# Stage A's second input passed in with its axes exchanged, and normalized, combined and loaded in that layout

## The chip, the cores and the metric

The kernel runs on one core of a Trainium2 chip. The metric is the time of one execution on the device in microseconds (us), smaller is better. A core has a matrix engine (TensorE, "PE" in the profile; its weight loads are "PEld"), three engines for elementwise work (VectorE "DVE", ScalarE "ACT", GpSimd "POOL"), and SyncE ("SP"), which here issues all transfers between main memory and the core's own memory, in its program order.

## The reference

All data are float32. x has two inputs (b = 0, 1) of 1024 tokens with 1024 features. Four blocks follow one another, each added to what it read:

```python
x = x + attention_a(layernorm(x))   # 32 heads of 32, causal, rotary, and a small adapter of 10 tokens
x = x + ffn(layernorm(x))           # base matrix, a router over 8 experts, rank-16 experts
x = x + attention_b(layernorm(x))   # 8 heads of 16 over all tokens
x = x + ffn(layernorm(x))           # the same weights again
```

Only the first block is touched. Its projection is, for each input,

```python
qkv = einsum('btc,oc->bto', layernorm(x), w_attn)    # 1024 x 1024 times 1024 x 3072
```

layernorm subtracts the mean of a token's 1024 features and multiplies by one over the root of their variance plus 1e-5.

## The kernel before

**Stage A.** The attention of 2 inputs x 8 groups of four heads x 2 halves of the queries is written as rounds (`attend`): each round issues scores, exponentials, and the products with v. Between the rounds goes other TensorE work, the "filler": a list of generators (`Filler`), from which each round takes steps worth 1990 ns by its own reckoning (`FILL_A`; a full matmul counts 512 x 1.7 = 870). The filler of stage A is the projection of q, k and v: one `project(b, g)` for each input and group, and behind them the output projection of input 0. `project(b, g)` waits until the attention of three groups earlier is done. TensorE's and GpSimd's orders are the order in which the program text issues; VectorE's, ScalarE's and SP's are arranged by a scheduler when the kernel is built. `pin_add`, `pin_sub` and `pin` put a VectorE operation behind the latest minimum of the attention's scores.

**Chores.** Small work for other engines is put into a queue (`fill.chore`), from which each filler step takes one; `flush(key)` empties the queue up to the last one of a name.

**The projection.** The weights lie in blocks `wqk` and `wv`. The normalized input lies in memory with features on the partitions and tokens along the rows, in two halves of 512 tokens: `xnT[b, n]`, 2 MB each, two buffers ("h16"). From group 1 on, a projection is done with seven block products instead of eight (`seven`): products 1, 6, 2, 7, 5, 4, 3, four matmuls of 128x512 each. Products 6, 7 and 4 read combinations of the halves (`td`, made once by `combine` and kept in main memory), which `Stream` fetches tile by tile into a ring of five buffers ("tt"). Product 1 and 2 read half 0; 5 and 3 read half 1. `factors` makes sums of the weights on VectorE. v is projected for two groups at once (`begin_values`, `values`), products 1, 6, 2, 7 with the even group and 5, 4, 3 with the odd one.

**Input 1.** In the course of groups 1 to 5 of input 0 (the arithmetic in 2 to 5) its eight tiles of 128 tokens are loaded ("xa", three buffers), normalized on VectorE, two at the start of a group (`normalize_ahead`, `layernorm`), and stored (`xnd`). In group 7 and the first projection of input 1 they are loaded again ("t4k", three buffers), and `second` flips each tile on TensorE (L204, eight transposes of 128x128, four to a PSUM bank), from where ScalarE or VectorE copies it to `xnT[1, n]` (L232, L234). `turn_over` spreads these transposes over the filler. Group 0 of input 1 is projected plainly (`project_first`): 2 halves x k and q x 8 matmuls. After each half `combine(1)` makes the combinations: VectorE for two, GpSimd for the third.

A matmul goes through `mm`, either as one of 128 columns (L198) or, between two rounds, as four of 32 columns side by side (L200).

Of the kernel before, what the change touches and what calls it, by code (L numbers as in the profile page):

```python
# [20 lines left out]
P = 128  # L21
B, T, C = 2, 1024, 1024
NT = T // P
# [18 lines left out]


AHEAD = "ahead"
WAIT = "wait"
# [102 lines left out]
def tile_model(ctx: ExitStack, tc: tile.TileContext, d, out: bass.AP):  # L148
# [92 lines left out]
    def layernorm(pl, tag, x, name, behind=False, then=None):  # L241
# [16 lines left out]
        e = pl.tile([P, 1], F32, tag="e0", name=f"e_{name}", bufs=2)  # L258
        xn = pl.tile([P, C], F32, tag=tag, name=f"xn_{name}")

        def rest():
            r = dve.tensor_scalar(e, r0, r0, ve, ALU.mult, ALU.mult)
            if behind:
                pin(r)
            dve.tensor_scalar(e, e, -0.5, 1.5, ALU.mult, ALU.add)
            dve.tensor_scalar(r0, r0, e, None, ALU.mult)
            dve.tensor_scalar(xn, x, mv[:, 0:1], r0, ALU.subtract, ALU.mult)  # L267
            if then is not None:
                then()
# [316 lines left out]

    xnd = [dram.tile([P, C], F32, name=f"xnd{t}") for t in range(NT)]

    def stage_a(wk, big):
# [46 lines left out]
        class Stream:  # L636


            def __init__(self, b, order):
                self.b, self.todo, self.here = b, deque((i, c) for i in order for c in range(4)), deque()  # L640
                self.fetch()

            def fetch(self):
                while self.todo and len(self.here) < RING:
                    i, c = self.todo.popleft()
                    t = big.tile([P, HF], F32, tag="tt", name=f"tt{self.b}_{i}_{c}_{len(self.todo)}")
                    sp.dma_start(t, td[self.b, i, c])
                    self.here.append(((i, c), t))

            def get(self, i, c):  # L650
                self.fetch()
                at, t = self.here.popleft()
                assert at == (i, c)
                return t

        streams = {}

# [5 lines left out]
        def combine(b):  # L663

            ts = {}
            for c in range(4):
                b11, b12, b21, b22 = (block(b, i)[:, c, :] for i in (11, 12, 21, 22))
                fill.chore(("T", b), lambda c=c, x=b22, y=b12: made(ts, b, 3, c, pin_sub, x, y))
                fill.chore(("T", b), lambda c=c, y=b11: made(ts, b, 2, c, pin_add, ts[3, c], y))
                fill.chore(("T", b), lambda c=c, y=b21: made(ts, b, 4, c, in_pieces(pool.tensor_sub), ts[2, c], y))  # L670

            order = []
            for g in range(NG):
                order += [2, 3, 4] if g else []
                if g > 1 or b:
                    order += [4] if g % 2 else [2, 3]
            fill.chore(("T", b), lambda: streams.update({b: Stream(b, order)}))

# [13 lines left out]
        def seven(b, nm, f, mul, shape, c, first, settled):  # L692
# [3 lines left out]
            right = {1: lambda k: block(b, 11)[:, k, :], 2: lambda k: block(b, 21)[:, k, :], 3: lambda k: block(b, 22)[:, k, :],  # L696
                     4: lambda k: streams[b].get(4, k), 5: lambda k: block(b, 12)[:, k, :],
                     6: lambda k: streams[b].get(2, k), 7: lambda k: streams[b].get(3, k)}

# [58 lines left out]

        def normalize_ahead():

            xs = {t: x_load(1, t, big, "xa") for t in range(2)}
            yield ("norm", -1)
            for t in range(NT + 1):
                if t:
                    settle(f"a1_{t - 1}")
                    sp.dma_start(xnd[t - 1], xn)
                if t + 2 < NT:
                    xs[t + 2] = x_load(1, t + 2, big, "xa")
                if t < NT:
                    xn = layernorm(big, "t4k", xs.pop(t), f"a1_{t}", behind=True)  # L770
                yield ("norm", t)

        def second():


            def load(t):
                xn = big.tile([P, C], F32, tag="t4k", name=f"xn1_{t}")
                sp.dma_start(xn, xnd[t])
                return xn

            xns = {t: load(t) for t in range(2)}
            for t in range(NT):
                n, i = divmod(t, 4)
                if i == 0:
                    yield None
                    xnT[1, n] = big.tile([P, NC, HF], F32, tag="h16", name=f"xnT1_{n}")
                if t + 2 < NT:
                    xns[t + 2] = load(t + 2)
                yield from transposed(xns.pop(t), xnT[1, n][:, :, i * P : (i + 1) * P], f"a1_{t}")

        given = [False]
        owed = [0]

        def turn_over():

            owed[0] += 1
            if given[0]:
                given[0] = False
                return
            while owed[0]:  # L800
                owed[0] -= 1
                yield next(turnover)

        def adapter_scores(u):
            given[0] = True
            b, g, n = u.at
# [32 lines left out]
        def late(r, begun):  # L839
            spent = 0.0  # L840
            given[0] = False
            for u, at in begun.items():
# [51 lines left out]
        def project(b, g, between=None):  # L894
# [5 lines left out]
            for key in "kq":  # L900
                st[key, b, g] = wk.tile([P, T], F32, tag="qk", name=f"{key}T{nm}")
            if g == 0:
                yield from project_first(b, between)
            else:
                yield from project_blocks(b, g)
            del wqk_at[b, g]
            if g and ng and nb < B:
                yield from begin(nb, ng)
            if (b, g) != (0, 0) and (b, g) != (0, 1):
                yield from values(b, g)  # L910

        def project_first(b, between):
            wqk = wqk_at[b, 0]
            if b == 0:
                yield adapter_parts("k0", lambda c: wqk[:, c, 1, :], P)
            else:
                assert next(turnover) is None
                yield from begin_values(b, 0)
            for n in range(2):
                if n == 1:  # L920
                    if b == 0:
                        yield from between
                    yield from begin(b, 1)
                    combine(b)
                xh = xnT[b, n]
                for s, key in ((1, "k"), (0, "q")):
                    qp = next_bank([P, HF], f"{key}p{b}_{n}")
                    for c in range(NC):
                        mm(qp, lhsT=wqk[:, c, s, :], rhs=xh[:, c, :], start=(c == 0), stop=(c == NC - 1))
                        yield HF * COL  # L930
                        if b and n == 0 and c % 2:
                            yield from turn_over()
                    rotate(b, 0, key, n, qp)
                    if b == 0 and n == 0 and key == "k":
                        yield adapter_keys(0)
                if b and n == 0:
                    while owed[0]:
                        owed[0] -= 1
                        yield next(turnover)
                yield ("qk", b, 0, n)  # L940
                if b == 0:
                    yield from values_first(n)
            combine_first(b)

        def project_blocks(b, g):
            nm = f"{b}_{g}"
            k, q = st["k", b, g], st["q", b, g]
            if (b, g) == (0, NG - 1):
                assert next(turnover) is None
            halves = {i: (t, n) for i, t, n in ((11, k, 0), (12, k, 1), (21, q, 0), (22, q, 1))}  # L950
# [10 lines left out]
            for r in seven(b, nm, st.pop(("f", b, g)), mul, [P, HF], places, lambda x: rotate(b, g, "k", 0, x), settled):  # L961
# [5 lines left out]
                else:  # L967
                    yield r
                    i += 1
                    if i == 14 and b == 0:  # L970
                        yield adapter_keys(g)
                    if (b, g) == (0, NG - 1) and i > 12 and i % 2 == 0:
                        yield from turn_over()
            while owed[0]:
                owed[0] -= 1
                yield next(turnover)
            yield ("qk", b, g, 1)
# [97 lines left out]
        fill.add(half(0, 0, xns))  # L1075
        ahead = normalize_ahead()
        turnover = second()
        for b in range(B):
            for g in range(NG):

                old = b * NG + g - 3
                if b == 0 and g >= 1:
                    fill.add(ahead_of(ahead, 2 if g > 1 else 1))
                fill.add(project(b, g, half(0, 1, xns) if b == g == 0 else None),
# [10 lines left out]
        return wp  # L1095

    def ahead_of(gen, n):
        for _ in range(n):
            r = next(gen, None)
            if r is not None:  # L1100
                yield r

# [533 lines left out]
    with tc.manual_schedule(engines={mybir.EngineType.PE}):  # L1636
        with tc.tile_pool(name="big", bufs=2, side="left", reuse_waits="tile") as bigp:
            psa = ExitStack()
            ps = psa.enter_context(tc.tile_pool(name="psA", bufs=1, space=bass.MemoryType.PSUM, reuse_waits="tile"))
            big = PoolOf(bigp, {"h16": 2, "t4k": 3, "xa": 3, "tt": RING, "wqk": 2, "wv": 1})  # L1640
            with tc.tile_pool(name="wkA", bufs=5, side="right", reuse_waits="tile") as wk:
# [163 lines left out]
```

## Time and profile before

| | |
|---|---|
| median of three runs | 2345.24 us (2343.0 to 2349.63) |
| the profiled execution | 2345.64 us, of which the profile's span is 2343.9 |
| TensorE busy | 2287.6 us (98%) |
| VectorE, ScalarE, GpSimd busy | 1435.9, 1090.6, 600.0 us |
| mean granted TensorE clock | 0.996 |
| projection and attention of stage A | about 19 to 1295 us; the hand-over from input 0 to input 1 near 580 us |

A line of the table by stretch gives start:end, length, then for PE, PEld, DVE, ACT and POOL the busy time with the number of instructions in brackets, then the granted clock (1.00 is full speed), the busy share of the transfer engines and GB/s. A line in order of time gives start, duration, engine, line of the program, operation, what it writes and reads, shapes, the number of instructions run together, and in square brackets how long the engine stood idle before it and for whom it waited. A line of the chain of waits gives start, duration and what. Lines of "PE" have modelled ends, so costs of matmuls are taken from start to start.

### The profile page before, as it was taken

To read this page: it belongs to the slowest core of one execution; us is meant where nothing else is said; L and a number is where in the kernel's file an instruction comes from. 1 tells how busy PE (TensorE), PEld (TensorE's weight loads), DVE (VectorE), ACT (ScalarE), POOL (GpSimd) and SP (SyncE) were. 2 spreads that over 40 slices of the span, in tenths; PEclk is the share of its full clock that TensorE was granted. 3 is DMA by queue.
4 is the path that set the end of the run, shared out by engine and by line. 5 is a ranking of instruction groups with operands and counts; after the bars stand their busy time and mean duration, and the time that the engine had idled before them with its cause. 6 is when DMAs were issued, how large, how long until landed. Compare 5 with 4: busy or idle time off the path is not lost.

```text
span 2343.9 us, 61203 instructions
## 1 busy us (share of the span) xinstructions
PE 2287.6 (98%) x25221; PEld 1048.8 (45%) x25221; DVE 1435.9 (61%) x4365; ACT 1090.6 (47%) x2090; POOL 600.0 (26%) x933
## 2 busy tenths in 40 slices
PE   8999999999999999999999999999999999999999
PEld 4435443455354443445433445566433553233454
DVE  7586766666656666566661246567766765675453
ACT  3356665666565665666652000012455545665100
POOL 1432232222233232222302114302111111222322
PEclk9999999999999999999999999999999999999999
DMA  5443334333243333332322574442332302323543
GB/s 175 151 140 117 121 102 129 110 96 111 88 124 110 103 98 108 91 111 80 128 73 78 192 249 171 157 144 79 127 104 84 118 19 73 117 82 112 180 161 123
DMA packets 182968, 277.37 MB, mean 118 GB/s; under 512 B 19488, under 2 KB 85152, under 8 KB 182688
## 3 DMA queue, kind: packets, MB, share of 16 engines
q1 hardware_dynamic: 182688, 273.46, 36.1%
q8 instruction: 197, 3.23, 0.6%
q14 instruction: 83, 0.68, 0.1%
HBM read 215.19 MB, written 55.57 MB: 116 GB/s over the span
## 4 chain that ended last, share of the span: by engine, by line
PE 87%; DVE 8%; DMA 3%; ACT 1%; issue 1%; POOL 0%; SPq 0%; DVEq 0%; POOLq 0%; ACTq 0%
PE st L411 9%; PE sc L339 7%; PE y_A L433 6%; PE y L200 6%; PE y_f L198 5%; PE x L200 4%; PE z_f L198 4%; PE z L200 4%; PE st L409 3%; PE y_v L200 3%; PE x_f L198 3%; PE y_B L433 2%; PE y_f L200 2%; PE y_p L198 2%; PE x_v L200 2%; PE hp_f L198 2%
## 5 line engine op out<-in xcount | busy, mean ns | idle before, releaser
L545 ACT ACTIVATE pt<-st 128x1024 f32<-128x1024 f32 (+1 forms) x418 | 424.0, 1019 | 559.7 <-PE st L411 433.3
L360 ACT ACTIVATE pr_A<-pr_A,nmax_A 128x896 f32<-128x896 f32 (+7 forms) x512 | 390.0, 765 | 43.5 <-DVE nmax_A L352 42.7
L352 DVE CUSTOM_DVE_ANT_0 pr_A<-sc,mask 128x512 f32<-128x512 f32 (+3 forms) x512 | 250.3, 536 | 179.0 <-PE st L411 96.4
L339 PE MATMUL sc<-kT,qT 32*128 32x512 f32 (+3 forms) x1536 | 319.3, 522 | 5.6 <-POOL qT L884 2.7
L411 PE MATMUL st<-qT,kT 32*128 32x512 f32 (+3 forms) x1536 | 297.0, 487 | 0.0
L352 DVE CUSTOM_DVE_ANT_0 pr_A<-sc,mask,part_A 128x512 f32<-128x512 f32 (+1 forms) x256 | 156.3, 648 | 146.5 <-PE sc L339 94.2
L418 POOL TENSOR_SCALAR_AFFINE_SELECT pt<-pt 128x256 f32<-128x256 f32 x256 | 104.4, 425 | 452.6 <-ACT pt L545 451.8
L239 POOL TENSOR_TENSOR xf<-xf,b_base 128x256 f32<-128x256 f32 x100 | 74.8, 779 | 413.4 <-DVE xn_f L267 288.4
L360 ACT ACTIVATE pr_B<-pr_B,nmax_B 128x1024 f32<-128x1024 f32 x128 | 145.5, 1140 | 35.4 <-DVE nmax_B L352 35.4
L433 PE MATMUL y_A<-pt,v 128*32 128x512 f32 (+3 forms) x1536 | 158.5, 498 | 1.8 <-issue 1.8
L339 PE MATMUL sc<-kq,qk 32*128 32x512 f32 x512 | 134.3, 643 | 6.6 <-DVE nmax_B L352 5.2
L411 PEld LDWEIGHTS st<-qT,kT 32*128 32x128 f32 x1536 | 129.1, 185 | 15.2 <-issue 10.7
L411 PE MATMUL st<-rows_B,kq 32*128 32x512 f32 x512 | 134.0, 640 | 1.1 <-ACT pt L545 0.8
L409 PE MATMUL st<-rows_A,ones 3*128 3x512 bf16 (+3 forms) x768 | 123.3, 329 | 4.7 <-DVE nmax_A L352 2.2
L352 DVE CUSTOM_DVE_ANT_0 pr_B<-sc,zeros,part_B 128x512 f32<-128x512 f32 x128 | 91.0, 747 | 51.8 <-PE sc L339 51.6
L409 PEld LDWEIGHTS <-ones 3*128 3x128 bf16 x768 | 35.9, 91 | 186.5 <-issue 181.0
L883 POOL TENSOR_TENSOR qr<-qr,sin 128x256 f32<-128x256 f32 x64 | 62.2, 972 | 220.2 <-DVE qr L879 213.4
L339 PEld LDWEIGHTS sc<-kT,qT 32*128 32x128 f32 x1536 | 109.9, 184 | 15.6 <-POOL qT L884 4.7
L352 DVE CUSTOM_DVE_ANT_0 pr_B<-sc,zeros 128x512 f32<-128x512 f32 x128 | 83.5, 686 | 52.9 <-PE sc L339 52.7
L200 PE MATMUL x<-xnT,wqk 128*32 128x512 f32 x896 | 109.6, 602 | 0.0
L200 PE MATMUL y<-tt,wqk 128*32 128x512 f32 x864 | 104.3, 594 | 0.0
L360 ACT ACTIVATION_READ_ACCUMULATOR pr_A<-pr_A,nmax_A 128x1 f32 x512 | 97.2, 190 | 0.0
(407 smaller groups left out, 4088.9 us busy)
## 6 DMA issues: line engine op xcount, KB each, us to landing
tt<-td SPq DMA_DIRECT2D x252, 256.0 KB
qkb_f<-tf SPq DMA_DIRECT2D x96, 256.0 KB
qkb_s<-tf SPq DMA_DIRECT2D x84, 256.0 KB
wqk<-in_w_attnT SPq DMA_DIRECT2D x32, 512.0 KB
xf<-x SPq DMA_DIRECT2D x25, 512.0 KB
xa<-in_x SPq DMA_DIRECT2D x16, 512.0 KB
wv<-in_w_attnT SPq DMA_DIRECT2D x8, 1024.0 KB
yd<-ys SPq DMA_DIRECT2D x32, 256.0 KB
```

Source lines behind the costliest of these rows:

```text
L198: return pe.matmul(out, lhsT=lhsT, rhs=rhs, start=start, stop=stop, skip_group_check=True)
L200: pe.matmul(out[i : i + 32], lhsT=lhsT[:, i : i + 32], rhs=rhs, start=start, stop=stop, skip_group_check=True)
L239: pool.tensor_add(dst[:, i : i + 2 * P], a[:, i : i + 2 * P], b[:, i : i + 2 * P])
L339: yield w * COL, lambda: pe.matmul(dst[:, o : o + w], lhsT=self.qt[rows, qc : qc + P], rhs=self.kt[rows, c0 : c0 + w], start=True, stop=True)
L352: minimum[0] = dve.tensor_tensor_reduce(pr[:, c0 : c0 + w], sc[:, i, o : o + w], m, -self.scale, BIG if c0 == 0 else self.part[:, col], AL ...
L360: tc.keep_in_program_order(act.activation(pr[:, :nk], pr[:, :nk], AF.Exp, bias=self.nmax[:, col], scale=-1.0, accum_out=self.sums[:, col]))
L409: yield w * COL / 4, lambda: pe.matmul(dst[:, o : o + w], lhsT=of["ones"][three, :], rhs=self.rows[three, off : off + w], start=True, stop ...
L411: yield w * COL, lambda: pe.matmul(dst[:, o : o + w], lhsT=self.kt[rows, kb * P : (kb + 1) * P], rhs=rhs, start=self.extra, stop=True)
L418: pool.affine_select(out=dg, in_=dg, compare_op=ALU.is_ge, fill=0.0, base=0, pattern=[[0, 2], [1, P]], channel_multiplier=-1)
L433: pe.matmul(self.y[32 * h : 32 * h + 32, off : off + w], lhsT=self.value(h, kb), rhs=pt[h // 2][:, h % 2, o : o + w], start=self.opens, st ...
L545: act.activation(pt[:, :, low_:wide_], st[:, :, low_:wide_], AF.Exp, scale=ts[0][0].scale)
L883: pool.tensor_mul(qr[:, hs], qr[:, hs], sin[:, cols][:, hs])
```

## The change

Input 1 is also passed in as `x1T`, its 1024 x 1024 values with features first. The eight loads by tokens stay, for mean and variance alone: `layernorm` with no tag ends with the two columns, which go to main memory (`moments`) in stores of 128 values. When all are there, they are loaded as two rows spread over all partitions ("mo", two tiles of 128x1024). Then, in four blocks c, two tiles of 128 features (c and c + 4, 128x1024 each) are loaded from `x1T` into "t4k"; VectorE subtracts the mean, GpSimd multiplies by the factor, and the three combinations for input 1 and the difference that product 5 needs are made there, one chore at each filler step; all are stored (`td`, `xnd`). The loads of block c + 1 are issued at the end of block c. `AHEAD_AT` says how many steps of this generator go ahead of a group's projection of q and k and how many behind it.

`second(n)` only loads: half 0 of input 1 into the buffer of half 0 of input 0 when product 2 of group 7 has read it, half 1 behind the last v product of group 7. There are no transposes, no copies and no `turn_over`. Group 0 of input 1 is projected in the seven-product form, and its first v products follow it like those of other even groups. One `Stream` runs over both inputs. "xa" (three buffers of 4 KB a partition) is gone; "mo" (two of 4 KB) and "z4" (one of 2 KB) are new.

```diff
+AHEAD_AT = {g: n for g, n in enumerate(((0, 0), (2, 0), (2, 2), (2, 1), (1, 1), (1, 1), (1, 1), (0, 0)))}
...
         def rest():
...
             dve.tensor_scalar(r0, r0, e, None, ALU.mult)
+            if xn is None:
+                then(mv[:, 0:1], r0)
+                return
             dve.tensor_scalar(xn, x, mv[:, 0:1], r0, ALU.subtract, ALU.mult)
...
-        def normalize_ahead():
...
+        def moments_ahead():
+            xs = {t: x_load(1, t, big, "t4k") for t in range(2)}
             yield ("norm", -1)
+            for t in range(NT):
                 if t + 2 < NT:
+                    xs[t + 2] = x_load(1, t + 2, big, "t4k")
+                def keep(mean, r, t=t):
+                    for i, v in enumerate((mean, r)):
+                        sp.dma_start(moments[i, t * P : (t + 1) * P].rearrange("(p o) -> p o", o=1), v)
+                settle(f"a1_{t - 2}")
+                layernorm(big, None, xs.pop(t), f"a1_{t}", behind=True, then=keep)
                 yield ("norm", t)
+            settle(f"a1_{NT - 1}")
+            mean, r = (big.tile([P, T], F32, tag="mo", name=f"moments{i}") for i in range(2))
+            for i, v in enumerate((mean, r)):
+                sp.dma_start(v, moments[i].partition_broadcast(P))
+            at = []
+            def load(c):
+                for k in (c, c + 4):
+                    x = big.tile([P, T], F32, tag="t4k", name=f"xc{k}")
+                    sp.dma_start(x, d["x1T"][k * P : (k + 1) * P, :])
+                    at.append(x)
+            load(0)
+            yield ("norm", NT)
+            for c in range(4):
...
+                for x, cols in places:
+                    chore(lambda x=x, cols=cols: pin_sub(x[:, cols], x[:, cols], mean[:, cols]))
+                for x, cols in places:
+                    chore(lambda x=x, cols=cols: in_pieces(pool.tensor_mul)(x[:, cols], x[:, cols], r[:, cols]))
+                    if x is hi:
+                        n = int(cols is right_)
+                        chore(lambda n=n, cols=cols, hi=hi: sp.dma_start(xnd[n, c + 4], hi[:, cols]))
+                chore(lambda: sp.dma_start(xnd[0, c], lo[:, left]))
+                chore(lambda: pin_sub(z[:, left], hi[:, right_], lo[:, right_]))
+                chore(lambda: pin_add(z[:, right_], z[:, left], lo[:, left]))
+                chore(lambda: in_pieces(pool.tensor_sub)(z4, z[:, right_], hi[:, left]))
+                chore(lambda: pin_sub(lo[:, right_], lo[:, right_], lo[:, left]))
+                def keep(c=c, lo=lo, z=z, z4=z4):
+                    sp.dma_start(td[1, 3, c], z[:, left])
+                    sp.dma_start(td[1, 2, c], z[:, right_])
+                    sp.dma_start(td[1, 4, c], z4)
+                    sp.dma_start(xnd[1, c], lo[:, right_])
+                    if c < 3:
+                        load(c + 1)
+                chore(keep)
+                yield ("norm", NT + 1 + c)
+                fill.flush("xc")
...
+        def second(n):
+            xnT[1, n] = big.tile([P, NC, HF], F32, tag="h16", name=f"xnT1_{n}")
+            for c in range(NC):
+                sp.dma_start(xnT[1, n][:, c, :], xnd[n, c])
...
-                yield from transposed(xns.pop(t), xnT[1, n][:, :, i * P : (i + 1) * P], f"a1_{t}")
...
             for key in "kq":
                 st[key, b, g] = wk.tile([P, T], F32, tag="qk", name=f"{key}T{nm}")
-            if g == 0:
-                yield from project_first(b, between)
+            if b == 0 and g:
+                yield from ahead_of(AHEAD_AT[g][0])
+            if b == g == 0:
+                yield from project_first(between)
             else:
                 yield from project_blocks(b, g)
             del wqk_at[b, g]
-            if g and ng and nb < B:
+            if (b or g) and nb < B:
                 yield from begin(nb, ng)
+            if b == 0 and g:
+                yield from ahead_of(AHEAD_AT[g][1])
             if (b, g) != (0, 0) and (b, g) != (0, 1):
                 yield from values(b, g)
+            if (b, g) == (0, NG - 1):
+                second(1)
...
-                    if (b, g) == (0, NG - 1) and i > 12 and i % 2 == 0:
-                        yield from turn_over()
+                    if (b, g) == (0, NG - 1) and i == 13:
+                        second(0)
...
-            big = PoolOf(bigp, {"h16": 2, "t4k": 3, "xa": 3, "tt": RING, "wqk": 2, "wv": 1})
+            big = PoolOf(bigp, {"h16": 2, "t4k": 3, "mo": 2, "z4": 1, "tt": RING, "wqk": 2, "wv": 1})
...
+        "x1T": a[A + "x"][1].T,
```

## The prediction

> **What bounds the kernel now.** I read the totals first, then the table by stretch, then the instructions in order of time on TensorE and VectorE, then the chain of waits around the hand-over from input 0 to input 1. The totals:
>
> ```profile
> PE 2287.6 (98%) x25221; PEld 1048.8 (45%) x25221; DVE 1435.9 (61%) x4365; ACT 1090.6 (47%) x2090; POOL 600.0 (26%) x933
> ```
>
> TensorE is the bound, and only 56 us are not its own. So an edit pays by the TensorE work it removes and by the gaps it closes, and it costs by the gaps it opens. The table by stretch shows where stage A has gaps (columns: length, then busy time of each engine, then granted clock):
>
> ```profile
> 125.00:145.00 20.00, 16.27 (x192) 5.62 (x188) 18.65 (x67) 9.17 (x33) 9.82 (x12) 1.00 0.65 215
> 195.00:216.00 21.00, 19.18 (x316) 9.66 (x306) 17.14 (x66) 14.62 (x41) 4.18 (x8) 0.92 0.37 117
> 276.00:296.00 20.00, 18.58 (x251) 7.31 (x244) 15.79 (x57) 12.97 (x33) 3.70 (x9) 1.00 0.56 193
> 355.00:376.00 21.00, 19.19 (x258) 7.88 (x254) 14.20 (x54) 11.86 (x28) 3.58 (x8) 0.92 0.62 205
> 376.00:440.00 64.00, 64.00 (x1000) 29.08 (x996) 40.91 (x131) 39.23 (x79) 19.43 (x30) 1.00 0.35 106
> 580.00:604.00 24.00, 18.42 (x192) 8.37 (x187) 12.18 (x38) 8.54 (x18) 2.91 (x8) 0.93 0.24 78
> ```
>
> The first four are the places where two layernorms of input 1 are pushed through VectorE. Their gaps are 3.73, 1.82, 1.42 and 1.81 us, and in two of them the clock of 0.92 costs another 21 x 0.08 = 1.7 us: 12.1 us in all, 3.0 for a pair. Between them, as in 376 to 440, TensorE never stops. The last row is the hand-over: 5.58 us idle and 24 x 0.07 = 1.7 us of clock.
>
> **Removed: 64 transposes on TensorE.** They come in 16 groups of four, one in nearly every round of attention:
>
> ```profile
> 539.71 1.07 PE L433 MATMUL y_A<-pt,v 128*32 128x512 f32 x8
> 540.70 0.66 PE L204 MATMUL xt_a<-ident,xn 128*128 128x128 f32 x4
> 541.20 1.02 PE L198 MATMUL z<-xnT,s 128*128 128x512 f32 x2
> ```
>
> From start to start a group takes 0.50 us, and the work ahead of it ends 0.11 us later than where no transpose follows (0.99 against 0.88 us for the same eight matmuls at 546.96). I take 0.60; a group behind a full-width matmul (559.13 to 559.57) took 0.44. So 16 x 0.60 = 9.6 us, at least 7.0. TensorE is never waiting for someone else there, so this is on the path.
>
> **Removed: four matmuls.** Group 0 of input 1 goes from 32 full matmuls to 28 of the seven-product form. Eight such matmuls take 3.43 us, so 4 x 0.43 = 1.7 us.
>
> **Removed: the stall at the hand-over.** Today the v weights of (1, 0) are loaded at 581.4, and the sums made of them stand next in VectorE's queue:
>
> ```profile
> 581.40 5.02 DMA wv<-in_w_attnT
> ```
> ```profile
> 582.19 0.68 DVE L730 TENSOR_TENSOR v<-v,z_v 128x512 f32<-128x512 f32 x1
> 586.44 0.69 DVE L227 TENSOR_TENSOR s_v<-wv 128x512 f32<-128x512 f32 x1 [3.57 <-DMA wv<-in_w_attnT]
> ```
> ```profile
> 589.03 0.63 PE L204 MATMUL xt_a<-ident,xn 128*128 128x128 f32 x4 [2.48 <-issue]
> 590.55 1.03 PE L204 MATMUL xt_a<-ident,xn 128*128 128x128 f32 x4 [0.89 <-DVE xnT L232]
> 598.36 0.66 PE L204 MATMUL xt_a<-ident,xn 128*128 128x128 f32 x4 [2.22 <-DVE rows_A L232]
> ```
>
> VectorE stands still for 3.57 us, and everything behind it (the copies of the transposes, the minima, rows_A) is late; TensorE loses 5.58 + 1.7 = 7.3 us. After the change the sums come behind 16 filler steps and there are no copies. A round of attention takes 3.9 us (624.43 to 628.33) and is given 1990 ns of filler at 870 for a step, 2.3 steps: 1.7 us a step, 27 us for the 16. The wait is covered. If it were not, 7.3 us stay. Removed in all: 18.6 us.
>
> [...] The rows decide: after a gap of 1.81 us at 204.7 the four us from 206 to 210 ran at 0.70.
>
> **Moved: the layernorms of input 1.** The statistics stay, the 0.81 us normalization on VectorE goes. A pair then costs 5.1 instead of 6.7 us of VectorE time. With 3.0 x 5.1 / 6.7 = 2.3 for each of four pairs it is 9.2 instead of 12.1: -2.9 us (between 0, if they crowd, since all are now done before group 4, and -6.4, if each pair falls to the cheapest, 1.42).
>
> **Added: four blocks of combination work**, one chore for each filler step, from the middle of group 4 to the start of group 6. Together 28 VectorE operations of 0.69 us (19.3) and 40 GpSimd pieces of about 0.75 us (30); gone are 7 copies, 8 normalizations and 8 sums on VectorE, 7 copies net on ScalarE. VectorE's sum rises by some 8 us with the nine operations of the new seven-product group, which lie where VectorE idles for TensorE (57.8 us busy of the 96 from 604 to 700). A block is 4.8 us of VectorE time; in one heap it would cost 3.0 x 4.8 / 6.7 = 2.2, but it is strung over some 27 us. I take 1.2 (between 0 and 3.5, the dearest later pair): 4.8 us.
>
> What speaks against it is that GpSimd slows VectorE where both work:
>
> ```profile
> 124.06 0.67 DVE L726 TENSOR_TENSOR qT<-qT,y 128x512 f32<-128x512 f32 x1
> 126.72 1.22 DVE L880 TENSOR_TENSOR qT<-qT,cos 128x512 f32<-128x512 f32 x1
> ```
>
> The second ran beside a GpSimd product (1.16 instead of 0.73 us). If all 28 ran so, they would add 28 x 0.54 = 15 us to VectorE, and a block would be 8.6 us, more than a pair: then 3.5 each. I hold 1.2, as most subtracts come before the products of their block.
>
> [...]
>
> **Added: waits for the new loads.** x1T comes as two 512 KB loads for each block into t4k's three slots, which the block before still fills; so block c+1 is loaded only when block c has stored. Blocks 0 and 2 follow their loads by 28 and 12 filler steps: no wait. Block 1 starts with the very step at which its load is issued (block 0 gets 19 chores and 17 steps). On SP ahead of that load stand a tt load that waits for TensorE, six awT transfers (0.53 to 0.66 us each, 3.6 us), a td store waiting for GpSimd; then it lands in 3.37 (512 KB, first x load of the chain) to 5.02 us (1 MB, above): 8.0 to 9.6 us. VectorE gets there after a round (3.9 us) and three operations, about 6 us: it waits 2 to 3.6 us. Queued behind it are the minima of the next round, for which ScalarE's exponentials wait, and for them TensorE, which has two sc buffers. By the hand-over's row: 3.0 us idle and 1.7 of clock, 4.7 us (0 to 7.3). Block 3 has one attention round and the four tail chores between load and use: 1.5 us (0 to 7.3). Together 6.2.
>
> **Added: SP's queue.** 54 more issues (16 small stores of mean and 1/deviation, 8 x1T loads, 2 broadcasts, 16 half loads for 8 whole ones, and so on), some 0.4 us each: 22 us over 400, no bound. But a store that waits for GpSimd holds the tt loads behind it. The ring of five covers about 8 steps, 14 us. Ends: 0, and 2.65 us for each block (the longest tt wait in the chain, at 150.71). I take 1.0 in all. The half loads of xnT at the hand-over go out 27 steps (half 0) and 16 steps (half 1) before use, against 15 us for 3 MB with the v weights at the 5.02 us row's rate; the tt load behind half 0 has 14 us for about 11.5: 0.5 us (0 to 2.65).
>
> **Sum.** -18.6 - 2.9 + 4.8 + 6.2 + 1.0 + 0.5 = -9.0 us. The profiled execution took 2345.64 us (span 2343.9), 0.4 above the median of 2345.24. So 2336.6 us.
>
> **The rivals.** *All gain:* blocks and loads hide, only the first two terms stand: -21.5, 2324.1 us. For it: 376 to 580 has 0.25 us of gap in 204. Against it: block 1's load.
> *No difference:* GpSimd stretches all VectorE work, blocks at 3.5 each (14.0 instead of 4.8): +0.2, 2345.8 us. For it the 1.22 row, against it that VectorE is idle a third of that time.
> *Slower:* each of the four blocks holds VectorE for its load as the v weights did, 4 x 7.3 = 29.2 instead of 6.2: +14.0, 2359.6 us. It decides once more than three of them wait in full (load waits over 22 us). Against it: the 28 and 12 steps ahead of blocks 0 and 2.
> That the transposes are not really gone is no rival: the changed program issues none for input 1.
>
> **How the numbers follow.** Chances: forecast 0.45 (2330 to 2342), all gain 0.17, no difference 0.22, slower 0.16. Under 0.3% (7 us, about what a measurement of this kernel tells from no change) counts as same; a sixth of the forecast's case lies there. Faster 0.38 + 0.17 = 0.55, same 0.07 + 0.22 = 0.29, slower 0.16. The range, 2324 to 2352, takes in the first three cases with their ends and leaves out most of the slower one.
>
> **What would show it.** Right: no gap around the hand-over, no xt_a group behind the start; one gap of 2 to 4 us at the start of group 5 (near 360 us), where VectorE waits for xc; small ones at groups 2 and 3. Wrong: VectorE waits for xc in all blocks, TensorE waits for tt or xnT, or the 128x512 subtracts last over 1 us and gaps line the stretch from 320 to 480.

## The result, and the profile after

The changed kernel takes 2366.8 us (median of 4 runs, 2359.09 to 2368.54), the kernel before 2347.24 beside it: a ratio of 1.0079, with a 95% interval of 1.0051 to 1.0107. It is slower by 20 us. The profiled execution took 2368.54 us, its span is 2366.8, the mean granted clock 0.988 (before 0.996). The totals of the page after:

```profile
PE 2287.3 (97%) x25263; PEld 1047.7 (44%) x25263; DVE 1448.4 (61%) x4378; ACT 1088.9 (46%) x2083; POOL 617.7 (26%) x957
```

TensorE's busy time is the same to 0.3 us, although the transposes are gone; the granted clock is lower, and with it back at 0.998 the best version below has 2267.4. The idle time rose from 56.3 to 79.5 us. The table by stretch, with the stretches of the prediction and, below them, two more:

```profile
125.00:145.00 20.00, 18.03 (x205) 6.01 (x200) 18.67 (x71) 9.97 (x35) 9.20 (x12) 0.91 0.90 137
195.00:216.00 21.00, 16.01 (x343) 10.71 (x342) 8.63 (x35) 12.86 (x29) 1.59 (x4) 0.92 0.58 90
276.00:296.00 20.00, 18.48 (x433) 12.00 (x428) 14.96 (x51) 12.15 (x25) 5.82 (x8) 1.00 0.59 96
355.00:376.00 21.00, 20.76 (x454) 12.71 (x448) 17.86 (x52) 14.37 (x31) 9.50 (x14) 1.00 0.38 110
376.00:440.00 64.00, 56.55 (x772) 23.56 (x768) 40.40 (x116) 32.95 (x63) 25.99 (x40) 0.92 0.50 165
580.00:604.00 24.00, 24.00 (x226) 6.94 (x218) 13.95 (x39) 13.51 (x22) 6.82 (x9) 1.00 0.46 150
145.00:195.00 50.00, 43.95 (x611) 17.62 (x604) 35.02 (x105) 22.89 (x46) 14.32 (x19) 0.93 0.56 99
480.00:500.00 20.00, 11.41 (x80) 3.85 (x83) 12.70 (x28) 5.83 (x10) 9.04 (x14) 0.66 0.37 124
```

The stall at the hand-over (580 to 604) is gone, as forecast. The stretch from 376, gapless before, now has 7.45 us of gap, and the one from 195 has 4.99 instead of 1.82. TensorE's larger gaps, in order of time (the bracket is the idle time ahead of the line and who ended it; one of 2.04 us at 235.79, behind VectorE, is left out):

```profile
153.85 3.64 PE L201 MATMUL y<-tt,wqk 128*32 128x512 f32 x16 [4.38 <-DMA tt<-td]
200.00 3.58 PE L201 MATMUL x_v<-wv,xnT 128*32 128x128 f32 x62 [2.98 <-issue]
251.49 1.93 PE L201 MATMUL y<-tt,wqk 128*32 128x512 f32 x8 [3.92 <-DMA tt<-td]
304.26 3.21 PE L201 MATMUL z_v<-wv,xnT 128*32 128x128 f32 x54 [5.18 <-issue]
400.21 1.22 PE L343 MATMUL sc<-kT,qT 32*128 32x512 f32 x2 [7.45 <-DVE part_A L356]
486.64 0.40 PE L413 MATMUL st<-rows_A,ones 3*128 3x256 bf16 x2 [6.81 <-DVE nmax_A L356]
490.68 0.39 PE L413 MATMUL st<-rows_A,ones 3*128 3x256 bf16 x2 [1.95 <-DVE rows_A L233]
```

They are of two kinds. Up to 305 us TensorE waits for combination tiles (tt) or for nothing that the profile shows ("issue"). At 400 and 487 it waits for VectorE, and VectorE waits for the x1T loads of blocks 1 and 3:

```profile
398.08 0.69 DVE L225 TENSOR_TENSOR xc<-xc,moments 128x512 f32<-128x512 f32 x1 [7.86 <-DMA xc<-in_x1T]
481.86 0.69 DVE L225 TENSOR_TENSOR xc<-xc,moments 128x512 f32<-128x512 f32 x1 [8.16 <-DMA xc<-in_x1T]
```

SyncE's queue ahead of the first of these loads (start, duration of the issue) and the chain of waits ahead of the second (start, duration, what) say why they are late:

```profile
388.66 0.55 SPq L868 DMA_DIRECT2D awTA<-adbA  x1
...
391.79 0.66 SPq L869 DMA_DIRECT2D awTA<-adbA  x1
392.54 0.38 SPq L817 DMA_DIRECT2D td<-xz  x1
392.97 1.86 SPq L788 DMA_DIRECT2D xc<-in_x1T  x2
```
```profile
469.34 7.36 DMA wv<-in_w_attnT
476.70 0.02 issue
476.72 5.02 DMA xc<-in_x1T
```

The first kind stands where the sixteen stores of means and factors are issued (92 to 290 us). Transfers are slow there: the chain of waits has one of the adapter's weights, 16 KB or less, that took 12.54 us. It spans the gap ahead of 153.85 and lands after it, so it is a neighbour of the late tt load and not its cause:

```profile
142.87 12.54 DMA awTA<-adbA
```

From 190 to 196 us, around two of the stores, the transfer engines are busy for 74% of the time and move 37 GB/s (last two columns):

```profile
190.00:196.00 6.00, 5.28 (x100) 2.57 (x94) 1.88 (x8) 1.03 (x1) 0.00 (x0) 1.00 0.74 37
```

A fixed mark serves for what follows: the last of the 32 stores of attention results (yd), where stage A's attention ends, at 1296.3 us before (first line) and at 1323.9 after (second).

```profile
L1046 SPq DMA_DIRECT2D yd<-ys x32: 319/378/834, 120.2 to 1296.3; - x32
L1066 SPq DMA_DIRECT2D yd<-ys x32: 319/376/982, 121.0 to 1323.9; - x32
```

Stage A lost 27.6 us. What follows took 1047.6 us before and 1042.9 after, with the same instructions; in the other profiled runs below it took 1038.4 to 1052.2. So a few us of a difference between whole times need not come from stage A; where a stage A price is wanted, the mark is better. The stores are counted from 0 here. Store 8 came 56.4 us later than before (510.2 against 453.8), store 16 only 26.6 later: 29.8 us of gains are there, behind larger losses. A store in the middle is a rougher mark than the last one, as it also moves with how much filler goes ahead of it.

### The profile page after: what moved, and what is told of

It reads as the page before. It is cut to its first block, busy times and chain, and to the rows that moved or that the text cites. A ratio compares the mean times of both kernels' runs of the same rounds, so it can differ in the third digit from the quotient of the medians.

```text
span 2366.8 us, 61406 instructions
## 1 busy us (share of the span) xinstructions
PE 2287.3 (97%) x25263; PEld 1047.7 (44%) x25263; DVE 1448.4 (61%) x4378; ACT 1088.9 (46%) x2083; POOL 617.7 (26%) x957
## 4 chain that ended last, share of the span: by engine, by line
PE 85%; DVE 7%; DMA 4%; ACT 2%; issue 1%; POOL 0%; SPq 0%; DVEq 0%; POOLq 0%; ACTq 0%
PE st L415 9%; PE sc L343 7%; PE y L201 6%; PE y_A L437 6%; PE y_f L199 4%; PE z L201 4%; PE x L201 4%; PE z_f L199 4%; PE st L413 3%; PE y_v L201 3%; PE x_f L199 3%; PE y_B L437 2%; PE y_f L201 2%; PE y_p L199 2%; PE z_v L201 2%; PE x_v L201 2%
## 5 line engine op out<-in xcount | busy, mean ns | idle before, releaser
L201 PE MATMUL y<-tt,wqk 128*32 128x512 f32 x960 | 118.9, 606 | 8.3 <-DMA tt<-td 8.3
L201 PE MATMUL x<-xnT,wqk 128*32 128x512 f32 x960 | 120.5, 614 | 0.0
L343 PEld LDWEIGHTS sc<-kT,qT 32*128 32x128 f32 x1536 | 110.6, 185 | 18.6 <-DVE part_A L356 8.0
```

Of the source, the lines that this page charges most:

```text
L201: pe.matmul(out[i : i + 32], lhsT=lhsT[:, i : i + 32], rhs=rhs, start=start, stop=stop, skip_group_check=True)
L343: yield w * COL, lambda: pe.matmul(dst[:, o : o + w], lhsT=self.qt[rows, qc : qc + P], rhs=self.kt[rows, c0 : c0 + w], start=True, stop=True)
```

## The experiments

Two theories. **T1:** the sixteen stores of 128 elements of 4 bytes clog the transfers, and tt, awT and instructions come late. **T2:** blocks 1 and 3 hold VectorE for loads that are issued too late. The rivals are crowded layernorms, a longer SyncE queue, and GpSimd slowing VectorE.

**One gathered store** (gather). The columns go to one tile, TensorE flips it, one store writes 16 rows of 512 bytes:

```diff
-    sp.dma_start(moments[i, t * P : (t + 1) * P].rearrange("(p o) -> p o", o=1), v)
+    dve.tensor_copy(cols[:, i * NT + t : i * NT + t + 1], v)
...
+            ct = bank([2 * NT, P], "colsT")
+            flip(ct, cols, ident)
+            rows = wk.tile([2 * NT, P], F32, tag="colsT", name="colsT_sb", bufs=1)
+            act.copy(rows, ct)
+            sp.dma_start(moments.rearrange("i (t p) -> (i t) p", p=P), rows)
```

> The changed kernel, but the means and factors of the eight layernorms are copied into sixteen columns of one SBUF tile, flipped once by TensorE and stored once as 16 rows of 512 bytes, instead of sixteen stores of 128 elements of 4 bytes. T1 (the small stores clog the DMA queues, and the tt and awT transfers and TensorE's instructions come late): the four gaps at 153.9 (4.38 us), 200.0 (2.98), 251.5 (3.92) and 304.3 (5.18) shrink to under 1.5 us each, awT and tt transfers in 125 to 300 land in under 5 us, and about 18 us of idle time and 8 us of clock go: some 2341 us where the changed kernel takes 2367. The gaps of 7.45 and 6.81 us at 400 and 487 stay. Rival (the pairs of layernorms crowd each other in groups 1 to 3, or SP has too many issues): the gaps stay, less than 5 us goes.

Measured: 2341.88 us, ratio to before 0.9979 (0.9971 to 0.9988); the four gaps are gone, the two others stay. T1 holds, 24.9 us below the changed kernel. The rivals of crowding and of SyncE's other new issues fall: those are all still there. TensorE's gaps over 0.9 us from 135 to 480 are now these:

```profile
182.42 0.39 PE L413 MATMUL st<-rows_A,ones 3*128 3x512 bf16 x2 [1.40 <-DVE part_A L356]
205.14 0.39 PE L413 MATMUL st<-rows_A,ones 3*128 3x512 bf16 x2 [1.22 <-DVE rows_A L233]
262.32 0.39 PE L413 MATMUL st<-rows_A,ones 3*128 3x512 bf16 x2 [1.51 <-DVE nmax_A L356]
368.87 1.22 PE L343 MATMUL sc<-kT,qT 32*128 32x512 f32 x2 [7.24 <-DVE part_A L356]
455.01 0.40 PE L413 MATMUL st<-rows_A,ones 3*128 3x256 bf16 x2 [6.38 <-DVE nmax_A L356]
459.05 0.40 PE L413 MATMUL st<-rows_A,ones 3*128 3x256 bf16 x2 [1.96 <-DVE rows_A L233]
```

**Blocks further apart** (spread). Only the values in the table of steps are changed:

```diff
-((0, 0), (2, 0), (2, 2), (2, 1), (1, 1), (1, 1), (1, 1), (0, 0))
+((0, 0), (3, 0), (2, 2), (2, 1), (1, 1), (0, 1), (0, 1), (1, 0))
```

> The changed kernel with the small stores kept, but the four combination blocks start at least 16 filler steps after their loads are issued (steps of the work ahead for groups 1 to 7: (3,0) (2,2) (2,1) (1,1) (0,1) (0,1) (1,0)). T2 (blocks 1 and 3 hold VectorE because the x1T load is issued with the step that uses it): VectorE no longer waits for xc, the gaps of 7.45 at 400 and of 6.81 and 1.95 at 487 go, and with the clock about 22 us: some 2345 us. Rival (GpSimd and VectorE slow each other in the blocks, and the gaps would be there with early loads too): gaps of 4 us or more stay at two blocks, and less than 8 us goes.

Measured: 2342.45 us, 0.9977 (0.9968 to 0.9986), 24.4 below the changed kernel. From 360 to 500 us VectorE waits for no load, and TensorE has no gap over 0.9 us behind 260. T2 holds. The gaps ahead of 260 stay, as the small stores do. The rival of GpSimd slowing VectorE falls: VectorE operations stretched beside GpSimd are still there, and no gap follows. One of them, and two stretches:

```profile
387.93 1.21 DVE L225 TENSOR_TENSOR xc<-xc 128x512 f32<-128x512 f32 x1
```
```profile
380.00:400.00 20.00, 20.00 (x330) 9.36 (x324) 15.22 (x50) 13.17 (x28) 7.28 (x14) 1.00 0.64 216
420.00:480.00 60.00, 60.00 (x988) 28.80 (x984) 43.73 (x132) 37.51 (x77) 28.67 (x44) 1.00 0.49 154
```

**Both** (both).

> One gathered store and spread blocks together. If T1 and T2 are the two causes and they are independent: 27 + 22 us less than the changed kernel, some 2318 us, 29 us below the kernel before, TensorE idle about 35 us. If one of them falls, the time is that of the other alone (2341 or 2345). If my forecast's remaining terms are right (-18.6 - 2.9 + 4.8 + 0.5, load waits at 0) it is 2329.

Measured: 2324.86 us, 0.991 (0.9897 to 0.9924): 22.7 us below before. Of the 27 + 22 expected, 42 came. Part of the rest is a gap that the gathering itself makes, where TensorE's flip waits for VectorE:

```profile
259.35 0.28 PE L205 MATMUL colsT<-ident,cols 128*16 128x128 f32 x1 [3.72 <-DVE parts_k L233]
```

**The flip later** (best). The same kernel, with the flip, its store and the broadcast loads as a chore five filler steps later:

```diff
+            for run in [lambda: None] * 5 + [gather]:
+                fill.chore("cols", run)
...
+            fill.flush("cols")
```

> The kernel with the gathered store and the spread blocks, with the flip of the sixteen columns, its store and the two broadcast loads five filler steps later, so that TensorE doesn't stand for 3.72 us at 259 behind VectorE's adapter copy. T: the gap goes and with it 216:276's clock of 0.97: 4 to 5.5 us, some 2320 us. Rival (the broadcast loads come too late for block 0 and VectorE waits for them): no gain or a loss of up to 3 us.

Measured: 2313.79 us, 0.987 (0.9852 to 0.9889). The gap is gone and the stretch's clock is back at 1.00:

```profile
216.00:276.00 60.00, 59.73 (x964) 27.69 (x951) 40.08 (x125) 38.21 (x75) 18.80 (x30) 1.00 0.37 113
```

By the mark it is 7.2 us ahead of the kernel with both (1267.5 against 1274.7), 5.5 of them already at store 3; the other 3.9 of the 11.1 between the medians are not in stage A's attention, and behind it the two have the same instructions.

```profile
L1078 SPq DMA_DIRECT2D yd<-ys x32: 319/380/1410, 120.3 to 1267.5; - x32
```

Against the changed kernel the mark moved by 56.4 us. T1 alone moved it by 32.5 (1291.4), T2 alone by 23.9 (1300.0): the two add up to the 56.4, which are the 27.6 lost and 28.8 gained on the kernel before. This version is 33 us faster than the kernel before and 53 faster than the changed one.

**The small stores alone, in the kernel before** (b_small). To a place that nobody reads:

```diff
                     sp.dma_start(xnd[t - 1], xn)
+                    for i in range(2):
+                        sp.dma_start(extra[i, t - 1, 0, :].rearrange("(p o) -> p o", o=1), last[f"a1_{t - 1}"][i])
```

> The kernel before, with two stores of 128 elements of 4 bytes added after each of the eight layernorms of input 1 (sixteen in all, the mean and the factor, to a place in DRAM that nobody reads); nothing else changed. T1: the stores alone cost 15 to 27 us, 2362 to 2374 us, with gaps of 3 us and more in 100 to 560 on TensorE that wait for tt or for instructions. Rival (the stores are harmless, as my forecast has it with at most 1 us): within 3 us of the kernel before.

Measured: 2396.96 us, 1.0216 (1.0202 to 1.023): +49.4, beyond the range. That is 49.4 / 16 = 3.1 us each, where the changed kernel's cost 24.9 / 16 = 1.6. These stores are spread over 123 to 412 us and may meet more tt loads; that was not tried. The chain of waits has a tt load of 256 KB that took 18.73 us, and TensorE's longest gap is the last line:

```profile
138.17 18.73 DMA tt<-td
156.89 0.04 issue
156.94 1.93 PE y L200 x8
```
```profile
346.71 1.93 PE L200 MATMUL y<-tt,wqk 128*32 128x512 f32 x8 [12.89 <-DMA tt<-td]
```

**What about them costs?** Four kernels with other sixteen stores at the same places (only the destination and the source of each store are given; a row of `extra` has 128 elements in b_far4 and 16 in b_step64):

```diff
-  extra[i, t - 1, 0, :].rearrange("(p o) -> p o", o=1), last[...][i]    # b_small: 128 x 4 B, side by side
+  extra[i, t - 1], xn[:, i * P : (i + 1) * P]                           # b_rows: 128 x 512 B
+  extra[i, t - 1], xn[:, i * 16 : (i + 1) * 16]                         # b_near64: 128 x 64 B, side by side
+  extra[i, t - 1][:, 0:1], last[...][i]                                 # b_far4: 128 x 4 B, 512 B apart
+  extra[i, t - 1][:, 0:1], last[...][i]                                 # b_step64: 128 x 4 B, 64 B apart
```

> The kernel before with sixteen added stores at the same places as the small ones, but each of 128 rows of 512 bytes (a slice of the normalized tile, 64 KB) to a place in DRAM that nobody reads. If the element size of 4 bytes is what costs, these stores with 128 times the bytes cost far less than the 49.4 us of the small ones: under 6 us, 2347 to 2354 us. If the number of issues or of rows, or SP's waiting behind a store, is what costs, they cost about the same: 2390 us or more.

> The kernel before with the sixteen added stores of 128 elements of 4 bytes, but each element goes to a row of its own, 512 bytes from the next, where the first such kernel put the 128 elements side by side. If the neighbourhood costs (many writers of one 512-byte stretch of DRAM wait for each other): under 8 us more than the kernel before. If the small element by itself costs: about the same 49 us, 2390 us or more.

> The kernel before with sixteen added stores of 128 rows of 64 bytes (sixteen columns of the normalized tile), side by side in DRAM, 8 KB each. If anything below 512 bytes costs like the 4-byte elements: about +49 us. If the cost belongs to elements of 4 bytes side by side, or falls with the size: under 10 us.

> The kernel before with the sixteen added stores of 128 elements of 4 bytes, each element 64 bytes from the next in DRAM. If the writers that hold each other up share a stretch of 64 bytes or less, these share none: under 8 us more than the kernel before, as with 512 bytes between them. If the shared stretch is longer (512 bytes, say), eight elements still fall into one: well over 10 us more, up to the 49 of side by side.

| sixteen stores, each of 128 pieces | median, us | ratio to the kernel before, run beside each |
|---|---|---|
| 4 B, side by side | 2396.96 | 1.0216 (1.0202 to 1.023) |
| 4 B, 64 B apart | 2347.31 | 1.0005 (0.9995 to 1.0016) |
| 4 B, 512 B apart | 2345.59 | 0.9996 (0.9985 to 1.0006) |
| 64 B, side by side | 2349.19 | 1.0006 (0.9994 to 1.0018) |
| 512 B, side by side | 2346.17 | 1.0 (0.9991 to 1.0009) |

T1 as I had put it, the 4-byte element, falls in part. Number of stores, of rows, small size and SyncE's issues cost nothing that can be measured here; of the five forms only the one with several elements within 64 bytes does (side by side there are sixteen in each such stretch; spacings between 4 and 64 bytes were not tried). The stretch from 136 to 160 us, first of the 4-byte elements side by side, then of those 512 B apart: fewer bytes, twice the share of the transfer engines.

```profile
136.00:160.00 24.00, 16.86 (x180) 6.19 (x174) 14.40 (x57) 10.96 (x34) 3.73 (x6) 0.89 1.04 144
```
```profile
136.00:160.00 24.00, 23.56 (x296) 7.67 (x292) 21.64 (x76) 14.29 (x41) 4.59 (x8) 0.97 0.51 161
```

If small size were what costs, the 64 B stores (2349.19 us) and the spaced 4 B stores (2347.31 and 2345.59) would have cost too. What happens in the memory when several elements go to one such stretch, no run here shows.

**From another queue** (act_small). In the changed kernel ScalarE issues the sixteen stores (`act.dma_start` for `sp.dma_start`).

> The changed kernel with its sixteen 4-byte-element stores issued from ScalarE instead of SyncE; nothing else changed. If the stores hold up what stands behind them in SyncE's queue alone: the tt gaps of 4.38 at 154 and 3.92 at 251 shrink, and 15 to 25 us of the 25 that the gathered store won are won here too, 2342 to 2352 us. If they clog the DMA engines for every queue: within 6 us of the changed kernel's 2366.8, and instruction fetches still come late.

Measured: 2367.65 us, 1.0086 (1.0068 to 1.0104), the changed kernel's time. So SyncE's order is not what holds the tt loads up. The gap at 251 is gone, but others came: one for tt at 111 (2.70 us), and the "issue" gap near 300 grew from 5.18 to 6.05.

```profile
154.33 3.90 PE L201 MATMUL y<-tt,wqk 128*32 128x512 f32 x16 [2.63 <-issue]
298.50 3.21 PE L201 MATMUL z_v<-wv,xnT 128*32 128x128 f32 x54 [6.05 <-issue]
```

This run has the small stores in a queue of their own, and shows that they do not fill the transfer engines themselves. Queue, packets, MB and share of the 16 engines' time, first of this run (SyncE's queue, then ScalarE's with the sixteen stores), then of SyncE's queue with the gathered store:

```profile
q1 hardware_dynamic: 188160, 281.85, 39.5%
q10 hardware_dynamic: 2304, 0.01, 0.1%
```
```profile
q1 hardware_dynamic: 188192, 281.86, 37.7%
```

The small stores' packets take 0.1%, 9 ns each in the median; SyncE's other packets, of the same bytes, take 1.8% more. In the traces' records of single packets, 109 in the changed kernel, 115 in spread, 136 here and 175 in b_small lasted over 2.5 us, nearly all of them packets of other transfers; none did in the ten kernels without such stores. A packet of 2 KB takes 84 ns in the median in all of them. So single packets of other transfers last up to 8.6 us in the changed kernel while these stores are about. What they wait for is not recorded.

**The hand-over alone** (b_late_wv). In the kernel before, the sums of the v weights wait until the first half is projected:

```diff
             for n in range(2):
                 if n == 1:
+                    if b:
+                        yield from begin_values(b, 0)
```

> The kernel before, with the seven-product sums of the v weights of input 1, group 0 placed after the first half's projection instead of ahead of it, some 16 filler steps after their load; nothing else changed. My forecast's term: VectorE's 3.57 us standstill at 582 goes, and TensorE's gaps of 2.48 and 2.22 us with it and the lowered clock: -7.3 us, 2340 us. Rival (the gaps there come from the transposes' copies and the start of the new input, whatever the weights do): less than 2 us.

Measured: 2347.15 us, 1.0005 (0.9995 to 1.0014): no gain, though VectorE's wait for wv at 582 (3.57 us) is gone. Store 12 comes at 607.0 instead of 611.8, 4.8 us ahead. Of the two gaps that I ascribed to that wait, the first is gone, the second is not (first line); and by store 13 the 4.8 are given back (664.6 against 663.0), at 640 to 665, where products now meet late minima and tt loads and the clock is 0.86. By the whole time the rival of my forecast holds.

```profile
593.59 0.66 PE L204 MATMUL xt_a<-ident,xn 128*128 128x128 f32 x4 [2.21 <-DVE rows_A L232]
647.86 0.70 PE L339 MATMUL sc<-kT,qT 32*128 32x512 f32 x2 [1.93 <-DVE nmax_A L352]
652.62 1.08 PE L200 MATMUL y_v<-s_v,tt 128*32 128x128 f32 x32 [1.41 <-DMA tt<-td]
654.85 1.93 PE L200 MATMUL y_v<-s_v,tt 128*32 128x128 f32 x32 [1.15 <-DMA tt<-td]
```

**The transposes' price** (both_flips). Dummy transposes in the kernel with both:

```diff
+   if (b, g) in ((0, NG - 1), (1, 0)) and i > 12 and i % 2 == 0:
+       pt = bank([P, 4, P], f"again_{b}_{i}")
+       for j in range(4):
+           flip(pt[:, j, :], ident, ident)
+       yield 440.0
```

> The kernel with the gathered store and the spread blocks, and sixteen groups of four transposes of the identity put in where the kernel before has its own for input 1 (group 7 of input 0 and the first projection of input 1), their results read by nobody. My forecast's price is 0.60 us a group: +9.6 us (7.0 at the least), 2334.5 us. Rival (TensorE has slack between the halves of a round, and the removed transposes gave less): under +4.

Measured: 2325.68 us, 0.9914 (0.9899 to 0.9929), only 0.8 above both. By whole times my price would fall. By the marks it stands: stores 16 to 20 come 8.8 to 9.9 us later than without the flips, 0.55 to 0.62 for a group, and the last store 7.0 later, my lower end. What lies behind stage A took 1038.4 us in this profile and 1049.3 in that of both. The difference is the clock and the gaps there, as the stretch from 1900 to 2300 us shows, first of both, then of this run:

```profile
1900.00:2300.00 400.00, 387.94 (x2584) 151.57 (x2585) 222.68 (x642) 165.19 (x264) 99.08 (x136) 0.98 0.36 119
```
```profile
1900.00:2300.00 400.00, 391.06 (x2639) 153.71 (x2640) 227.38 (x656) 169.16 (x269) 103.05 (x142) 1.00 0.36 120
```

TensorE idles 12.1 us in the first and 8.9 in the second, and 400 x 0.02 = 8 us go to the clock in the first alone. What lowers the clock there in one run and not in the other is open, so the price is shown for stage A, and not as a change of the whole time.

## Why the prediction was wrong

**The step that failed first: "SP's queue", "16 small stores ... some 0.4 us each ... no bound", 1.0 us in all.** I priced the stores by what their issue costs SyncE and by who queues behind them. What I had at 1.0 cost 24.9 us by the medians (32.5 by the mark): not SyncE's time and not its order (issued from ScalarE they cost the same), but packets of other transfers that lasted over 2.5 us beside them, 109 of them, up to 8.6. The trace of before held no row of such a store, and I gave it no upper end of its own; its bounds were those of the tt wait (2.65 for each of four blocks). The destination, 128 neighbouring values, was in the diff.

**The second: "load waits", 6.2 us**, with 4.7 for block 1 and 1.5 for block 3. The mechanism was right, as were the six awT transfers ahead of the load. The term measured 24.4 us by the medians (23.9 by the mark). The load of block 1 landed as late as forecast: 9.4 us from the first awT issue at 388.66 to the subtract at 398.08, against 8.0 to 9.6. But I let VectorE come after a round and three operations, some 6 us. It stood there from 398.08 - 7.86 = 390.22, ahead of the load's issue at 392.97, as the subtract of block 1 is next in its queue behind the last of block 0. At block 3 I put a round and four chores between load and use; VectorE stood there from 481.86 - 8.16 = 473.70, ahead of the issue at 476.72, and I missed a 1 MB load of v weights ahead of x1T in the queue. My own upper end, 7.3 for a wait, was a hand-over with 3.57 us of standstill; this one lasts twice as long, and the exponentials and TensorE stop behind it.

**The range** ended at 2352 and left out most of the slower rival. That rival, 2359.6, came near in time and by its own sign: load waits over 22 us decide for it, and they were 24.4. But two blocks waited, some 12 us each, and not four at 7.3; and it has nothing of the stores' 24.9.

**What was right.** With both causes removed the mark is 28.8 us ahead of before; my terms without load waits and SyncE's queue make -18.6 - 2.9 + 4.8 + 0.5 = -16.2. The parts:

- Transposes, -9.6: 7.0 to 9.9 by the dummy flips.
- Hand-over, -7.3: the gap and its clock are gone in the changed kernel. The wait for wv explains 4.8 of it at store 12 by the experiment, which lost them again right behind; the gap behind rows_A (2.22 us) has another cause, and went with the plain projection and its copies, which I did not separate.
- Four matmuls, -1.7: not tried by itself.
- Layernorm pairs, -2.9: where I counted 12.1 us of gaps and clock before, the best version has gaps of 0.98, 0.99, 1.40 and 1.22 us and 20 x 0.09 = 1.8 of clock, 6.4 in all. That is -5.7, near my outer bound of -6.4. (Its store 8 is 6.4 ahead of before, its store 10 only 2.7, with 0.23 us of gap from 376 to 525 in both kernels: there a store's place follows the filler.)
- Combination blocks, +4.8: nothing. With the loads early, 380 to 400 and 420 to 480 show no gap, as the "all gain" rival had it; the 1.2 us rows cost TensorE nothing, as VectorE idles there for about a quarter of the time (15.22 of 20 and 43.73 of 60 us busy). A subtract beside GpSimd's work took 1.21 us (387.93 in spread), the same one at 461.94 took 0.68, but no time followed from it.
- xnT hand-over, +0.5: no gap there.

With 7.0 to 9.9 for the transposes, 1.7, 7.3 and 5.7 make 21.7 to 24.6 of the 28.8, the 1.7 untried. In the rest is a gap of 1.80 us that before has at 660.10 and the best version has not.

**The clock.** The prediction counted a lowered clock beside short gaps, by its rows (1.81 us of gap, then 0.70 from 206 to 210). The rows held again: from 125 to 145 us the best version has two gaps of 0.98 and 0.99 us, 18.03 us busy, and a clock of 0.91. That every gap lowers it is not shown: the kernel before has 3.73 us without TensorE in the same stretch at 1.00.

## What to carry to other kernels

Price a new transfer by its destination too: a column of 128 partitions stored to neighbouring 4-byte places is 128 writes to eight stretches of 64 bytes, and cost 1.6 to 3.1 us of the whole kernel each, through the transfers around it; flip the columns together and store rows (24.9 us less here than the changed kernel), or space the elements by 64 bytes (2347.31 us where side by side took 2396.96). When a load is issued at the end of one block and first used at the start of the next, ask what the consuming engine has in between: if the next instruction in its queue is the use, the whole landing time and all that stands ahead on the issuing queue is a standstill (7.86 and 8.16 us here). And mark fixed events (here the 32 result stores) in both traces, so that gains behind a loss can be seen.

## What was not expected of the hardware

- Sixteen stores of 512 bytes each, less than 10 KB in all, cost 49.4 us, while sixteen of 64 KB cost nothing that could be measured.
- Such a store delays transfers on other queues as well (issued from ScalarE, at the changed kernel's full price): its own packets take 9 ns, those of others up to 8.6 us in the changed kernel. TensorE's gaps without a visible cause, 5.18 us at 304 in the changed kernel, went with them. That instructions came late there, as T1 has it, is argued and not shown: from 296 to 305 us the records have one packet of an instruction queue (q8) among 494, and do not say whether TensorE waited for it.
- The part behind stage A, with the same instructions, took 1038.4 to 1052.2 us in the profiled runs. Where two of them were laid side by side, the clock and the gaps made the difference (0.98 and 12.1 us idle against 1.00 and 8.9 in one stretch of 400); what brings them on is open.
